# Batch statistics of a bottleneck's last convolution: a pass over its output against the Gram matrix of its input

## The chip, the cores and the metric

The kernel runs on one core of a Trainium2 chip. The metric is device time of one execution in microseconds (us). One execution of the kernel was also recorded by the hardware profiler; all rows below come from that one. Everything is computed in f32.

## The reference

Two residual blocks follow each other on x of shape 64 x 1024 x 14 x 14, each with parameters of its own. The reference of one block, cut to what matters:

```python
def _conv(x, w, b, stride, pad):
    y = jax.lax.conv_general_dilated(x, w, window_strides=(stride, stride), padding=[(pad, pad), (pad, pad)], dimension_numbers=('NCHW', 'OIHW', 'NCHW'))
    return y + b.reshape(1, -1, 1, 1)

def _bn(x, gamma, beta):
    mean = jnp.mean(x, axis=(0, 2, 3), keepdims=True)
    var = jnp.var(x, axis=(0, 2, 3), keepdims=True)
    xn = (x - mean) * jax.lax.rsqrt(var + EPS)
    return gamma.reshape(1, -1, 1, 1) * xn + beta.reshape(1, -1, 1, 1)

out = jax.nn.relu(_bn(_conv(x, w1, b1, 1, 0), g1, be1))     # 1x1, 1024 -> 256 channels
out = jax.nn.relu(_bn(_conv(out, w2, b2, 1, 1), g2, be2))   # 3x3, 256 -> 256
out = _bn(_conv(out, w3, b3, 1, 0), g3, be3)                # 1x1, 256 -> 1024
out = jax.nn.softplus(residual_scale)[0] * out
return jax.nn.relu(x + out)
```

Mean and variance are taken over all 64 x 14 x 14 = 12544 pixels of a channel, so a convolution must be finished for all images before its result can be normalized.

## The kernel before

Channels lie on the 128 partitions: the 1024 channels in 8 slots of a partition (CS), the 256 in 2 (MS). Images are taken two at a time, so that a tile has 392 pixels (PX) and there are 32 tiles (T). The 256 channels of all images stay in on-chip memory through a block, as tiles y0 to y31 that each stage rewrites in place. The 1024 channels of all images do not fit on chip.

A block goes through these stages, each a loop over the 32 tiles:

- conv1: 8 slots of x against w1, for two output slots. ScalarE moves the result out of PSUM with its bias into y (L92), VectorE takes its statistics (L93, one set per tile).
- conv2: ScalarE normalizes y into a padded tile (L99; three pad tiles in turn, NPAD), TensorE runs nine taps x two slots for each output slot (L108), ScalarE moves the result into y (L114), VectorE takes statistics (L115).
- norm2_conv3_stats: ScalarE normalizes y in place (L127), TensorE runs conv3 for all eight output slots (L120), and VectorE takes statistics straight out of PSUM (L129). The products themselves are dropped.
- residual: x is loaded again (SP's queue), conv3 runs once more (L120), VectorE multiplies it by the scale and adds x (L138), ScalarE adds the shift and applies the relu (L141), and POOL's queue stores the tile (L143): in the first block to a buffer in DRAM (mid), in the second to the output. In the first block each tile goes on into the next block's conv1 from where it lies.

Between two stages, affine aggregates the tiles' statistics (L158) and works out scale and shift in small operations (L160 to L177). x tiles share four buffers, PSUM is eight banks with one tile each. The order within an engine and all signals come from a scheduler that works on the program as written; it tracks which operation reads or writes which tile.

Of the kernel before, what the change touches and what calls it, by code (L numbers as in the profile page):

```python
"""Two ResNet bottleneck blocks (1x1 -> 3x3 -> 1x1 convolutions, each with batch statistics) in NCHW.

Channels lie on partitions: channel c of 1024 is partition c // 8, slot c % 8, and channel c of 256 is
partition c // 2, slot c % 2, so that an image's rows of a partition are contiguous in DRAM. The 256
channels of all images stay in SBUF through a block, a tile for every two images; each stage rewrites
these tiles in place. The last convolution runs twice: for its statistics, and again where its result
is added to the residual, as its 1024 channels do not fit on chip. Where the first block ends, its
result feeds the next block's first convolution straight from SBUF.
"""

# [1 line left out]

# [4 lines left out]

FP = mybir.dt.float32
AF = mybir.ActivationFunctionType
ALU = mybir.AluOpType  # L20

P = 128
N, C, H, W = 64, 1024, 14, 14
HW = H * W
M = 256  # channels between the 1x1 convolutions
CS = C // P  # slots of a partition with 1024 channels
MS = M // P  # and with 256
G = 2  # images in a tile
T = N // G
PX = G * HW  # L30
HP, WP = H + 2, W + 2
TAPS = [(i, j) for i in range(3) for j in range(3)]
EPS = 1e-5
NPAD = 3

# Columns of a block's packed parameters.
B1, G1, BE1, B2, G2, BE2 = (MS * i for i in range(6))
B3, G3, BE3 = (6 * MS + CS * i for i in range(3))
RS = 6 * MS + 3 * CS
NPAR = RS + 1  # L40


@with_exitstack
def bottlenecks(ctx: ExitStack, tc: tile.TileContext, x, w1s, w2s, w3s, pars, out):
    nc = tc.nc
# [3 lines left out]
    keep = ctx.enter_context(tc.tile_pool(name="keep", bufs=1))  # L49
    wpool = ctx.enter_context(tc.tile_pool(name="weights", bufs=1))  # L50
    xpool = ctx.enter_context(tc.tile_pool(name="x", bufs=4))
    small = ctx.enter_context(tc.tile_pool(name="small", bufs=2))
    psum = ctx.enter_context(tc.tile_pool(name="psum", bufs=8, space=bass.MemoryType.PSUM))
    dram = ctx.enter_context(tc.tile_pool(name="dram", bufs=1, space=bass.MemoryType.DRAM))

    ys = [keep.tile([P, MS, PX], FP, tag=f"y{t}", name=f"y{t}") for t in range(T)]
    pads = [keep.tile([P, MS, G, HP, WP], FP, tag=f"pad{i}", name=f"pad{i}") for i in range(NPAD)]
    mids = [dram.tile([P, G, CS * HW], FP, tag=f"mid{t}", name=f"mid{t}") for t in range(T)]

# [17 lines left out]
        nc.sync.dma_start(out=xt.rearrange("p i s f -> p i (s f)"), in_=x_t[t] if b == 0 else mids[t])  # L77
        return xt

    def psum_tile():  # L80
        return psum.tile([P, PX], FP, tag="ps", name="ps")

    def conv1(xt, t, w1, par, stats):
        for o in range(MS):
# [32 lines left out]
    def conv3(t, o, w3):  # L117
        ps = psum_tile()
        for s in range(MS):
            nc.tensor.matmul(ps, w3[:, s, o, :], ys[t][:, s, :], start=(s == 0), stop=(s == MS - 1))  # L120
        return ps

    def norm2_conv3_stats(t, w3, aff, stats):
        scale, shift = aff
        for s in range(MS):
            y = ys[t][:, s, :]
            nc.scalar.activation(y, y, AF.Relu, bias=shift[:, s : s + 1], scale=scale[:, s : s + 1])  # L127
        for o in range(CS):
            nc.vector.bn_stats(stats[:, o, t, :], conv3(t, o, w3))  # L129

    def residual(b, t, w3, aff):
        """relu(x + scale * conv3 + shift), in place of x."""
        scale, shift = aff
        xt = load_x(b, t)
        for o in range(CS):
            ps = conv3(t, o, w3)
            v = xt[:, :, o, :]
            nc.vector.scalar_tensor_tensor(  # L138
                v, ps.rearrange("p (i f) -> p i f", i=G), scale[:, o : o + 1], v, ALU.mult, ALU.add
            )  # L140
            nc.scalar.activation(v, v, AF.Relu, bias=shift[:, o : o + 1])  # L141
        to = mids[t] if b == 0 else out_t[t]
        nc.gpsimd.dma_start(out=to, in_=xt.rearrange("p i s f -> p i (s f)"))  # L143
        return xt

    def stats_tile(n, name):
        return keep.tile([P, n, T, nc.vector.BN_STATS_DIM], FP, tag=f"stats{n}", name=name)

    def affine(stats, n, par, g, be, conv_bias=None):
        """scale and shift with scale * y + shift = g * (y - mean) / sqrt(var + EPS) + be, for y  # L150
        with the statistics, or for y + conv_bias where that is given."""

        def tl(name):
            return small.tile([P, n], FP, tag=f"{name}{n}", name=name)

        mv = small.tile([P, n, nc.vector.BN_AGGR_DIM], FP, tag=f"mv{n}", name="mv")
        for o in range(n):
            nc.vector.bn_aggr(mv[:, o, :], stats[:, o, :, :].rearrange("p t f -> p (t f)"))  # L158
        v, sd, r, q = tl("v"), tl("sd"), tl("r"), tl("q")
        nc.vector.tensor_scalar(v, mv[:, :, 1], EPS, None, ALU.add)  # L160
        nc.scalar.activation(sd, v, AF.Sqrt)  # L161
        nc.vector.reciprocal(r, sd)
        # One Newton step on r = v ** -0.5.
        nc.vector.tensor_mul(q, r, r)
        nc.vector.tensor_mul(q, q, v)
        nc.vector.tensor_scalar(q, q, -0.5, 1.5, ALU.mult, ALU.add)
        nc.vector.tensor_mul(r, r, q)
        scale, shift, off = tl("scale"), tl("shift"), tl("off")
        nc.vector.tensor_mul(scale, r, par[:, g : g + n])
        if conv_bias is None:  # L170
            nc.vector.tensor_scalar(off, mv[:, :, 0], -1.0, None, ALU.mult)
        else:
            bias = par[:, conv_bias : conv_bias + n]
            nc.vector.tensor_add(off, mv[:, :, 0], bias)
            nc.vector.tensor_sub(off, bias, off)
        nc.vector.tensor_mul(shift, off, scale)
        nc.vector.tensor_add(shift, shift, par[:, be : be + n])  # L177
        return scale, shift

    def softplus(par):  # L180
        """max(a, 0) + log1p(exp(-|a|))"""
        a = par[:, RS : RS + 1]

        def tl(name):
            return small.tile([P, 1], FP, tag=name, name=name)

        u, w, l, d, z = tl("u"), tl("w"), tl("l"), tl("d"), tl("z")
        nc.vector.tensor_scalar(u, a, -1.0, None, ALU.mult)  # L188
        nc.vector.tensor_tensor(u, u, a, ALU.min)  # L189
        nc.scalar.activation(u, u, AF.Exp)  # L190
        # log1p(u) = log(w) * u / (w - 1) with w = 1 + u rounded, and u where w is 1.
        nc.vector.tensor_scalar(w, u, 1.0, None, ALU.add)
        nc.scalar.activation(l, w, AF.Ln)
        nc.vector.tensor_scalar(d, w, 1.0, None, ALU.subtract)
        nc.vector.tensor_scalar(z, d, 0.0, None, ALU.is_equal)
        nc.vector.tensor_add(d, d, z)
        nc.vector.reciprocal(d, d)
        nc.vector.tensor_mul(l, l, d)
        nc.vector.tensor_add(l, l, z)
        nc.vector.tensor_mul(l, l, u)  # L200
        sp = tl("sp")
        nc.vector.tensor_scalar(sp, a, 0.0, None, ALU.max)
        nc.vector.tensor_add(sp, sp, l)
        return sp

# [1 line left out]
    w1 = load_w1(0)  # L207
    par = []
    for b in range(2):
        p = keep.tile([P, NPAR], FP, tag=f"par{b}", name=f"par{b}")  # L210
        nc.scalar.dma_start(out=p, in_=pars[b])
        par.append(p)
    for pad in pads:
        nc.gpsimd.memset(pad, 0.0)  # L214

    stats1 = stats_tile(MS, "stats1_0")
    for t in range(T):
        conv1(load_x(0, t), t, w1, par[0], stats1)
        if t == 2:
            w2, w3 = load_w2(0), load_w3(0)  # L220
    w1 = load_w1(1)

    for b in range(2):
        pb = par[b]
        sp = softplus(pb)
        aff = affine(stats1, MS, pb, G1, BE1)
        stats2 = stats_tile(MS, f"stats2_{b}")
        for t in range(T):
            conv2(t, w2, pb, aff, stats2)

        aff = affine(stats2, MS, pb, G2, BE2)
        stats3 = stats_tile(CS, f"stats3_{b}")
        for t in range(T):
            norm2_conv3_stats(t, w3, aff, stats3)
        if b == 0:
            w2 = load_w2(1)

        aff = affine(stats3, CS, pb, G3, BE3, conv_bias=B3)
        for a in aff:
            nc.vector.tensor_scalar(a, a, sp, None, ALU.mult)  # L240
        if b == 1:
            for t in range(T):
                residual(b, t, w3, aff)
            return
        stats1 = stats_tile(MS, f"stats1_{b + 1}")
        ahead = residual(b, 0, w3, aff)
        for t in range(T):
            xt, ahead = ahead, residual(b, t + 1, w3, aff) if t + 1 < T else None
            conv1(xt, t, w1, par[b + 1], stats1)
        w3 = load_w3(b + 1)  # L250
# [35 lines left out]
```

## Time and profile before

| | |
|---|---|
| median of 3 runs | 3594.09 us (3593.11 to 3594.46) |
| span of the profiled execution | 3593.3 us |
| granted TensorE clock, mean | 0.996 |
| TensorE matmul busy | 3552.1 us (99%) |
| VectorE busy | 794.0 us (22%) |
| ScalarE busy | 635.1 us (18%) |
| HBM read, written | 163.09 MB, 102.76 MB |

Rows name an engine (PE is TensorE's matmuls, PEld its weight loads, DVE is VectorE, ACT is ScalarE, POOL is GpSimd, SP is SyncE), a line of the kernel, the operation and its operands by the program's names, as in out<-in. A group row gives, after the count, busy time and mean duration, then the idle time just before its instructions and what ended it. A timeline row begins with start and length in us. Matmuls overlap each other in TensorE, so the mean duration of one is longer than the distance between two.

### The profile page before, as it was taken

To read this page: it belongs to the slowest core of one execution; us is meant where nothing else is said; L and a number is where in the kernel's file an instruction comes from. 1 tells how busy PE (TensorE), PEld (TensorE's weight loads), DVE (VectorE), ACT (ScalarE), POOL (GpSimd) and SP (SyncE) were. 2 spreads that over 40 slices of the span, in tenths; PEclk is the share of its full clock that TensorE was granted. 3 is DMA by queue.
4 is the path that set the end of the run, shared out by engine and by line. 5 is a ranking of instruction groups with operands and counts; after the bars stand their busy time and mean duration, and the time that the engine had idled before them with its cause. 6 is when DMAs were issued, how large, how long until landed. Compare 5 with 4: busy or idle time off the path is not lost.

```text
span 3593.3 us, 24805 instructions
## 1 busy us (share of the span) xinstructions
PE 3552.1 (99%) x10752; PEld 2043.4 (57%) x10752; DVE 794.0 (22%) x1394; ACT 635.1 (18%) x1037; POOL 42.7 (1%) x71
## 2 busy tenths in 40 slices
PE   8999999999999999999999999999999999999998
PEld 5555555555555555555555555555555555555555
DVE  1111000000002444422322320000000034445444
ACT  1111011101104000222322221101111040003444
POOL 0000000000000000000000000000000000000000
PEclk9999999999999999999999999999999999999999
DMA  6444000000000000244333430000000000005886
GB/s 236 155 153 164 0 0 0 1 0 0 0 0 27 0 0 1 94 157 153 152 152 153 159 140 0 0 0 0 0 0 1 0 0 0 0 0 212 299 299 264
DMA packets 36589, 267.44 MB, mean 74 GB/s; under 512 B 2944, under 2 KB 2944, under 8 KB 27520
## 3 DMA queue, kind: packets, MB, share of 16 engines
q1 hardware_dynamic: 22592, 160.96, 12.6%
q0 software_dynamic: 13312, 102.76, 6.9%
q10 hardware_dynamic: 576, 2.14, 0.2%
q8 instruction: 84, 1.38, 0.2%
q14 instruction: 25, 0.20, 0.0%
HBM read 163.09 MB, written 102.76 MB: 74 GB/s over the span
## 4 chain that ended last, share of the span: by engine, by line
issue 90%; PE 9%; POOL 1%; DMA 0%; POOLq 0%
PE ps L87 9%; POOL out L143 1%; POOL mid L143 0%; DMA x<-in_x 0%; POOLq L143 0%; POOLq L280 0%
## 5 line engine op out<-in xcount | busy, mean ns | idle before, releaser
L108 PE MATMUL ps<-pad,w 128*128 128x392 f32 x4608 | 1522.7, 493 | 10.3 <-ACT pad L99 10.3
L120 PE MATMUL ps<-y,w 128*128 128x392 f32 x4096 | 1357.1, 493 | 10.3 <-ACT y L127 10.3
L108 PEld LDWEIGHTS ps<-pad,w 128*128 128x128 f32 x4608 | 873.4, 190 | 659.6 <-ACT pad L99 11.5
L120 PEld LDWEIGHTS ps<-y,w 128*128 128x128 f32 x4096 | 779.6, 190 | 582.9 <-ACT y L127 12.2
L87 PE MATMUL ps<-x,w 128*128 128x392 f32 x2048 | 682.3, 494 | 9.9 <-DMA x<-in_x 9.9
L87 PEld LDWEIGHTS ps<-x,w 128*128 128x128 f32 x2048 | 390.4, 191 | 296.0 <-issue 12.6
L115 DVE BATCH_NORM_STATS2 stats<-y 128x6 f32<-128x392 f32 x128 | 72.9, 569 | 1452.0 <-ACT y L114 1452.0
L138 DVE SCALAR_TENSOR_TENSOR x<-ps,scale,x 128x392 f32<-128x392 f32 x512 | 319.2, 625 | 328.8 <-PE ps L120 325.1
L141 ACT ACTIVATE x<-x,shift 128x392 f32<-128x392 f32 x512 | 317.5, 622 | 373.4 <-DVE x L138 373.3
L129 DVE BATCH_NORM_STATS2 stats<-ps 128x6 f32<-128x392 f32 x512 | 293.0, 572 | 376.6 <-PE ps L120 376.6
L114 ACT ACTIVATE y<-ps,par 128x392 f32<-128x392 f32 x128 | 75.2, 587 | 1060.4 <-PE ps L108 1060.4
L93 DVE BATCH_NORM_STATS2 stats<-y 128x6 f32<-128x392 f32 x128 | 72.8, 569 | 616.1 <-ACT y L92 616.1
L92 ACT ACTIVATE y<-ps,par 128x392 f32<-128x392 f32 x128 | 75.2, 587 | 577.0 <-PE ps L87 577.0
L99 ACT ACTIVATE pad<-y,shift,scale 128x392 f32<-128x392 f32 x128 | 89.8, 709 | 309.5 <-PE ps L108 306.2
L161 ACT ACTIVATE sd<-v 128x2 f32<-128x2 f32 (+1 forms) x6 | 1.2, 205 | 614.4 <-DVE v L160 614.4
L127 ACT ACTIVATE y<-y,shift,scale 128x392 f32<-128x392 f32 x128 | 77.6, 699 | 3.2 <-DVE shift L177 3.2
L143 POOL DMA_DIRECT2D mid<-x x32 | 17.2, 537 | 2095.1 <-ACT x L141 2095.1
L143 POOL DMA_DIRECT2D out<-x x32 | 22.6, 707 | 1446.5 <-ACT x L141 1446.5
L158 DVE BATCH_NORM_AGGREGATE mv<-stats 128x2 f32<-128x192 f32 x24 | 24.5, 1022 | 0.8
L188 DVE TENSOR_SCALAR u<-par 128x1 f32<-128x1 f32 x2 | 0.3, 154 | 11.7 <-DMA par<-in_par 11.7
L214 POOL MEMSET pad<- 128x1024 f32 x3 | 2.7, 952 | 0.3 <-POOLq L274 0.3
L190 ACT ACTIVATE u<-u 128x1 f32<-128x1 f32 x2 | 0.4, 202 | 8.7 <-DVE u L189 8.7
(33 smaller groups left out, 18.7 us busy)
## 6 DMA issues: line engine op xcount, KB each, us to landing
x<-in_x SPq DMA_DIRECT2D x64, 1568.0 KB, 6.5
mid<-x POOLq DMA_DIRECT2D x32, 1568.0 KB, 5.4
x<-mid SPq DMA_DIRECT2D x32, 1568.0 KB, 8.4
out<-x POOLq DMA_DIRECT2D x32, 1568.0 KB, 10.6
w<-in_w SPq DMA_DIRECT2D x2, 2304.0 KB, 14.9
w<-in_w ACTq DMA_DIRECT2D x2, 1024.0 KB, 7.2
w<-in_w SPq DMA_DIRECT2D x2, 1024.0 KB, 14.0
par<-in_par ACTq DMA_DIRECT2D x2, 18.5 KB, 9.5
```

The source lines that it names most:

```text
L87: nc.tensor.matmul(ps.rearrange("p (i f) -> p i f", i=G), w1[:, s, o, :], xt[:, :, s, :], start=(s == 0), stop=(s == CS - 1),)
L92: nc.scalar.activation(y, ps, AF.Identity, bias=par[:, B1 + o : B1 + o + 1])
L99: nc.scalar.activation(pad[:, s, :, 1 : H + 1, 1 : W + 1], ys[t][:, s, :].rearrange("p (i h w) -> p i h w", i=G, h=H), AF.Relu, bias=shift ...
L108: nc.tensor.matmul(ps.rearrange("p (i h w) -> p i h w", i=G, h=H), w2[:, s, k, o, :], pad[:, s, :, i : i + H, j : j + W], start=(s == 0 an ...
L114: nc.scalar.activation(y, ps, AF.Identity, bias=par[:, B2 + o : B2 + o + 1])
L115: nc.vector.bn_stats(stats[:, o, t, :], y)
L120: nc.tensor.matmul(ps, w3[:, s, o, :], ys[t][:, s, :], start=(s == 0), stop=(s == MS - 1))
L127: nc.scalar.activation(y, y, AF.Relu, bias=shift[:, s : s + 1], scale=scale[:, s : s + 1])
L129: nc.vector.bn_stats(stats[:, o, t, :], conv3(t, o, w3))
L138: nc.vector.scalar_tensor_tensor(v, ps.rearrange("p (i f) -> p i f", i=G), scale[:, o : o + 1], v, ALU.mult, ALU.add)
L141: nc.scalar.activation(v, v, AF.Relu, bias=shift[:, o : o + 1])
L143: nc.gpsimd.dma_start(out=to, in_=xt.rearrange("p i s f -> p i (s f)"))
```

## The change

The statistics of conv3 no longer come from running conv3. Its output is linear in its input z (the normalized, relu'd y), so the mean of an output channel is w . mean(z), and its variance is w' G w less the square of that, with G the 256 x 256 matrix of the mean products of z's channels. To keep the numbers small, a constant per channel, max(be2, 0), is first subtracted from z.

- gram: z is taken in 49 steps of 256 pixels. Each step transposes four blocks of 128 x 128 on TensorE into one PSUM tile (two chunks of 128 pixels, two slots), VectorE subtracts the constant on the way out of PSUM into one of four tiles zt, and two accumulated products a chunk follow: 257 columns (the first slot against everything and a column of ones) and 129 columns (the second slot against itself and the ones). The products of a step stand behind the transposes of the next.
- conv3_stats: G is scaled and moved out of PSUM, multiplied by w3 (six matmuls of 512 columns), by w3 again on VectorE, and summed over partitions with matmuls of one column; the means come from matmuls of two columns. The result takes the place of the aggregated statistics, and affine is otherwise as before.
- All y tiles become views of one tile, and there are two pads instead of three. The packed parameters grow by 256 columns (the constant along a row). Their identity and ones are set up on POOL at the start. A tile q of the statistics shares the four x buffers.

The core of the diff:

```diff
-NPAD = 3
+NPAD = 2
+NPX = N * HW
+CH = 2
+NT = NPX // (CH * P)
+NZT = 4
...
-    ys = [keep.tile([P, MS, PX], FP, tag=f"y{t}", name=f"y{t}") for t in range(T)]
+    y_all = keep.tile([P, MS, NPX], FP, tag="y", name="y")
+    ys = [y_all[:, :, t * PX : (t + 1) * PX] for t in range(T)]
+    zts = [keep.tile([P, CH, M + 1], FP, tag=f"zt{i}", name=f"zt{i}") for i in range(NZT)]
+    ident = keep.tile([P, P], FP, tag="ident", name="ident")
...
-    def norm2_conv3_stats(t, w3, aff, stats):
+    def norm2(t, aff):
         scale, shift = aff
         for s in range(MS):
             y = ys[t][:, s, :]
             nc.scalar.activation(y, y, AF.Relu, bias=shift[:, s : s + 1], scale=scale[:, s : s + 1])
+
+    def gram(aff, crow):
+        g0 = psum.tile([P, 512], FP, tag="ps", name="g0")[:, : M + 1]
+        g1 = psum.tile([P, 512], FP, tag="ps", name="g1")[:, : P + 1]
+        normed = 0
+
+        def products(k, zt):
+            for c in range(CH):
+                first, last = k == 0 and c == 0, k == NT - 1 and c == CH - 1
+                nc.tensor.matmul(g0, zt[:, c, 0:P], zt[:, c, :], start=first, stop=last)
+                nc.tensor.matmul(g1, zt[:, c, P:M], zt[:, c, P:], start=first, stop=last)
+
+        before = None
+        for k in range(NT):
+            while normed * PX < (k + 1) * CH * P:
+                norm2(normed, aff)
+                normed += 1
+            tp = psum_tile(CH * M)
+            for c in range(CH):
+                px = slice((k * CH + c) * P, (k * CH + c + 1) * P)
+                for s in range(MS):
+                    nc.tensor.transpose(tp[:, (c * MS + s) * P : (c * MS + s + 1) * P], y_all[:, s, px], ident)
+            zt = zts[k % NZT]
+            nc.vector.tensor_tensor(
+                zt[:, :, :M], tp.rearrange("p (c m) -> p c m", c=CH),
+                crow[:, None, :].to_broadcast([P, CH, M]), ALU.subtract,
+            )
+            if before is not None:
+                products(*before)
+            before = k, zt
+        products(*before)
+        return g0, g1
+
+    def conv3_stats(grams, w3, ccol, mv):
+        g0p, g1p = grams
...
+        nc.vector.tensor_scalar(g0, g0p, 1.0 / NPX, None, ALU.mult)
+        nc.scalar.activation(g1, g1p, AF.Copy, scale=1.0 / NPX)
+        nc.vector.tensor_scalar(off, g0[:, P:M], 2.0, None, ALU.mult)
...
+        half = CS // 2
+        q = xpool.tile([P, MS, C], FP, tag="x", name="q")
+        for h in range(2):
+            cols = slice(h * half, (h + 1) * half)
+            t0, t1 = psum_tile(half * P), psum_tile(half * P)
+            nc.tensor.matmul(t0, g0[:, 0:P], w3[:, 0, cols, :], start=True, stop=True)
+            nc.tensor.matmul(t1, off, w3[:, 0, cols, :], start=True, stop=False)
+            nc.tensor.matmul(t1, g1[:, 0:P], w3[:, 1, cols, :], start=False, stop=True)
+            for s, t in ((0, t0), (1, t1)):
+                nc.vector.tensor_mul(
+                    q[:, s, h * half * P : (h + 1) * half * P], t, w3[:, s, cols, :].rearrange("p o c -> p (o c)")
+                )
         for o in range(CS):
-            nc.vector.bn_stats(stats[:, o, t, :], conv3(t, o, w3))
+            for s in range(MS):
+                nc.tensor.matmul(quad[:, o, 0:2], w3[:, s, o, :], m[:, s, :], start=(s == 0), stop=(s == MS - 1))
+        for o in range(CS):
+            for s in range(MS):
+                nc.tensor.matmul(quad[:, o, 2:3], q[:, s, o * P : (o + 1) * P], ones, start=(s == 0), stop=(s == MS - 1))
...
-        aff = affine(stats2, MS, pb, G2, BE2)
-        stats3 = stats_tile(CS, f"stats3_{b}")
-        for t in range(T):
-            norm2_conv3_stats(t, w3, aff, stats3)
+        aff = affine(aggregate(stats2, MS), MS, pb, G2, BE2)
+        grams = gram(aff, crow)
         if b == 0:
             w2 = load_w2(1)
 
-        aff = affine(stats3, CS, pb, G3, BE3, conv_bias=B3)
+        mv3 = small.tile([P, CS, nc.vector.BN_AGGR_DIM], FP, tag="mv3", name="mv3")
+        conv3_stats(grams, w3, ccol, mv3)
+        aff = affine(mv3, CS, pb, G3, BE3, conv_bias=B3)
```

More of the change, by code (lines that the diff above doesn't have):

```diff
@@ L14 @@
 import concourse.tile as tile
-from concourse import mybir
+from concourse import masks, mybir
 from concourse._compat import with_exitstack
@@ L40 @@
 NPAR = RS + 1
+NROW = M
 @with_exitstack
@@ L78, in load_x, with psum_tile @@
         return xt
-    def psum_tile():
-        return psum.tile([P, PX], FP, tag="ps", name="ps")
+    def psum_tile(n=PX):
+        return psum.tile([P, 512], FP, tag="ps", name="ps")[:, :n]
     def conv1(xt, t, w1, par, stats):
@@ new lines, in conv3_stats @@
+    def conv3_stats(grams, w3, ccol, mv):
+        g0p, g1p = grams
+        g0 = keep.tile([P, M + 1], FP, tag="g0", name="g0")
+        g1 = keep.tile([P, P + 1], FP, tag="g1", name="g1")
+        off = keep.tile([P, P], FP, tag="goff", name="goff")
+        nc.vector.tensor_scalar(g0, g0p, 1.0 / NPX, None, ALU.mult)
+        nc.scalar.activation(g1, g1p, AF.Copy, scale=1.0 / NPX)
+        nc.vector.tensor_scalar(off, g0[:, P:M], 2.0, None, ALU.mult)
+        m = keep.tile([P, MS, 2], FP, tag="zmean", name="zmean")
+        for s, d in ((0, g0[:, M:]), (1, g1[:, P:])):
+            nc.vector.tensor_copy(m[:, s, 1:2], d)
+            nc.vector.tensor_add(m[:, s, 0:1], d, ccol[:, s : s + 1])
+        quad = psum_tile(3 * CS).rearrange("p (o k) -> p o k", k=3)
+        ones = keep.tile([P, 1], FP, tag="ones", name="ones")
+        nc.vector.memset(ones, 1.0)
+        half = CS // 2
[10 more added lines that the diff above has]
+                )
+        for o in range(CS):
+            for s in range(MS):
[3 more added lines that the diff above has]
+                nc.tensor.matmul(quad[:, o, 2:3], q[:, s, o * P : (o + 1) * P], ones, start=(s == 0), stop=(s == MS - 1))
+        r = small.tile([P, CS, 3], FP, tag="quad", name="quad")
+        nc.vector.tensor_copy(r, quad)
+        nc.vector.tensor_copy(mv[:, :, 0], r[:, :, 0])
+        sq = small.tile([P, CS], FP, tag="sq", name="sq")
+        nc.vector.tensor_mul(sq, r[:, :, 1], r[:, :, 1])
+        nc.vector.tensor_sub(mv[:, :, 1], r[:, :, 2], sq)
@@ L147, in stats_tile, with aggregate @@
         return keep.tile([P, n, T, nc.vector.BN_STATS_DIM], FP, tag=f"stats{n}", name=name)
-    def affine(stats, n, par, g, be, conv_bias=None):
-        def tl(name):
-            return small.tile([P, n], FP, tag=f"{name}{n}", name=name)
+    def aggregate(stats, n):
         mv = small.tile([P, n, nc.vector.BN_AGGR_DIM], FP, tag=f"mv{n}", name="mv")
@@ L158, in affine, with tl @@
             nc.vector.bn_aggr(mv[:, o, :], stats[:, o, :, :].rearrange("p t f -> p (t f)"))
+        return mv
+    def affine(mv, n, par, g, be, conv_bias=None):
+        def tl(name):
+            return small.tile([P, n], FP, tag=f"{name}{n}", name=name)
         v, sd, r, q = tl("v"), tl("sd"), tl("r"), tl("q")
@@ L209, in bottlenecks @@
     for b in range(2):
-        p = keep.tile([P, NPAR], FP, tag=f"par{b}", name=f"par{b}")
+        p = keep.tile([P, NPAR + NROW], FP, tag=f"par{b}", name=f"par{b}")
         nc.scalar.dma_start(out=p, in_=pars[b])
@@ L214, in bottlenecks @@
         nc.gpsimd.memset(pad, 0.0)
+    for zt in zts:
+        nc.gpsimd.memset(zt[:, :, M:], 1.0)
+    masks.make_identity(nc, ident)
     stats1 = stats_tile(MS, "stats1_0")
@@ L225, in bottlenecks @@
         sp = softplus(pb)
-        aff = affine(stats1, MS, pb, G1, BE1)
+        crow = keep.tile([P, M], FP, tag="crow", name="crow")
+        nc.vector.tensor_scalar(crow, pb[:, NPAR:], 0.0, None, ALU.max)
+        ccol = keep.tile([P, MS], FP, tag="ccol", name="ccol")
+        nc.vector.tensor_scalar(ccol, pb[:, BE2 : BE2 + MS], 0.0, None, ALU.max)
+        aff = affine(aggregate(stats1, MS), MS, pb, G1, BE1)
         stats2 = stats_tile(MS, f"stats2_{b}")
@@ L264, in packed @@
         cols.append(np.broadcast_to(get("residual_scale").reshape(1, 1), (P, 1)))
+        cols.append(np.broadcast_to(get("be2").reshape(P, MS).T.reshape(1, M), (P, M)))
         w1 = get("w1").reshape(P, MS, P, CS).transpose(2, 3, 1, 0)
```

## The prediction

> **What bounds the kernel now.** The page comes first: which engine is full, and whether it is full all the way.
>
> ```profile
> span 3593.3 us, 24805 instructions
> ...
> PE 3552.1 (99%) x10752; PEld 2043.4 (57%) x10752; DVE 794.0 (22%) x1394; ACT 635.1 (18%) x1037; POOL 42.7 (1%) x71
> ...
> PE   8999999999999999999999999999999999999998
> ```
>
> TensorE is busy in every slice, and no other engine passes 22%. Whatever leaves TensorE's list shortens the run, as long as no other engine is slow in the stage that takes its place. The waits say how little TensorE stands still:
>
> ```profile
> PE ps L120 <- ACT y L127: 10.3, 2, 5.2
> ...
> PE ps L108 <- ACT pad L99: 10.3, 2, 5.2
> PE ps L87 <- DMA x<-in_x: 9.9, 1, 9.9
> ```
>
> About 30 us in all: the first load, and four stage starts of 5.2 us each, at which the statistics of the stage before must be finished first. Then the busy time by stage; the third and the sixth stretch are the statistics passes of the two blocks, and the last is the second block's residual.
>
> ```profile
> 1117.00:1463.00 346.00, 341.41 (x1032) 196.98 (x1033) 156.85 (x276) 39.12 (x66) 0.00 (x0) 1.00 0.02 7
> ...
> 2915.00:3255.00 340.00, 340.00 (x1035) 196.24 (x1034) 157.38 (x280) 33.09 (x56) 0.00 (x0) 1.00 0.00 0
> 3255.00:3593.00 338.00, 327.56 (x996) 188.74 (x994) 156.06 (x250) 155.34 (x250) 22.61 (x32) 0.99 0.77 286
> ```
>
> The columns are length, busy time and instructions of PE, PEld, DVE, ACT and POOL, then the granted clock, the DMA share and GB/s. In a statistics pass TensorE is full and VectorE less than half full. The groups give its pieces:
>
> ```profile
> L120 PE MATMUL ps<-y,w 128*128 128x392 f32 x4096 | 1357.1, 493 | 10.3 <-ACT y L127 10.3
> L120 PEld LDWEIGHTS ps<-y,w 128*128 128x128 f32 x4096 | 779.6, 190 | 582.9 <-ACT y L127 12.2
> ...
> L138 DVE SCALAR_TENSOR_TENSOR x<-ps,scale,x 128x392 f32<-128x392 f32 x512 | 319.2, 625 | 328.8 <-PE ps L120 325.1
> ...
> L129 DVE BATCH_NORM_STATS2 stats<-ps 128x6 f32<-128x392 f32 x512 | 293.0, 572 | 376.6 <-PE ps L120 376.6
> L114 ACT ACTIVATE y<-ps,par 128x392 f32<-128x392 f32 x128 | 75.2, 587 | 1060.4 <-PE ps L108 1060.4
> ...
> L99 ACT ACTIVATE pad<-y,shift,scale 128x392 f32<-128x392 f32 x128 | 89.8, 709 | 309.5 <-PE ps L108 306.2
> ```
>
> L120 serves the statistics pass and the residual, in each of two blocks: 4 x 32 tiles x 8 outputs x 2 slots = 2048 matmuls in the code and 4096 records here. So one f32 matmul is two records, each with a weight load of its own. The mean of 493 ns is a latency; the pace comes from the timeline of an undisturbed stretch:
>
> ```profile
> 1120.82 19.46 ACT L127 ACTIVATE y<-y,shift,scale 128x392 f32<-128x392 f32 x32 [1.61 <-DVE shift L177]
> ...
> 1139.81 326.37 PE L120 MATMUL ps<-y,w 128*128 128x392 f32 x991
> ```
>
> 326.37 / 991 = 0.329 us for a record of 392 columns, that is 0.84 ns a column, and 0.493 - 0.329 = 0.16 us of latency that is hidden in a stream.
>
> **The change, part by part.**
>
> *Removed.* In each block 32 x 8 x 2 = 512 matmuls, 1024 records x 0.3293 = 337.2 us, all on the path. The 256 BATCH_NORM_STATS2 and 8 aggregations on VectorE go too, but they lie beside TensorE and are worth nothing.
>
> *Added: products.* 49 steps a block, each with two chunks of 128 pixels. A chunk has a product of 257 columns (two records of 257 x 0.84 = 0.216 us) and one of 129 (two of 0.108 us), if the weight load keeps up. All matmuls of the trace are long, so loads always hide. Two loads issued into an idle array show what a load by itself holds up:
>
> ```profile
> 2906.47 0.19 PEld L120 LDWEIGHTS ps<-y,w 128*128 128x128 f32 x1 [5.78 <-ACT y L127]
> ...
> 2906.47 0.30 PEld L120 LDWEIGHTS ps<-y,w 128*128 128x128 f32 x2 [5.78 <-ACT y L127]
> ```
>
> The second load ends 0.30 us after the start of the first and takes 0.19 itself, so it began 0.11 us after it: a load of 0.19 us lets the next begin after 0.11. I take 0.11 as the floor for a short record; the other end is the whole 0.19. Products per step: 4 x 0.216 + 4 x 0.11 = 1.30 us.
>
> *Added: transposes.* Four of 128x128 a step. No row shows one. The lower end is one record each with its load wholly hidden and at half a product's price by column, 128 x 0.84 / 2 = 0.054 us, a guess at the most that leaving the products out can save. The upper is two records at 0.19. I take one record at the load's 0.11, nearest to the row just shown, because moving values through the array has no sum of products that would have to be split: 0.44 us a step. If it is split like every f32 product here, it is 0.88.
>
> The Trainium skill, "TensorE: Matmul & The Clock Gate", Terms, says that transpose mode makes f32 four times faster on trn2. Against two records of 0.108 us that would be 0.054 us, below the floor of the load, so the sum by it would be the one taken here.
>
> *One step* is 1.30 + 0.44 = 1.74 us, and 49 steps are 85.5 us a block.
>
> *What lies beside it.* VectorE's one subtraction of 512 columns out of PSUM a step: six operations of 392 columns there, back to back, take
>
> ```profile
> 1463.46 0.17 DVE L160 TENSOR_SCALAR v<-mv 128x8 f32<-128x8 f32 x1
> ...
> 1465.75 3.40 DVE L138 SCALAR_TENSOR_TENSOR x<-ps,scale,x 128x392 f32<-128x392 f32 x6
> ```
>
> 0.57 us each. With 0.17 us of that fixed, as for the operation of 8 columns above them, and the rest 1.02 ns a column, 512 columns cost 0.69 us. The products of a step are issued after the next step's transposes, so the subtraction has 1.74 us for 0.16 (array) + 0.69: hidden. ScalarE's normalization runs at 19.46 / 32 = 0.61 us an operation, 1.22 a tile; a step needs 256 / 392 of one, 0.79 us: hidden too. If the step ran at half its length, VectorE would be late next.
>
> *Start of the stage.* Before, TensorE began behind the first normalization. Now the first products need two of them, a transpose and the subtraction, and the second transposes need the next tile, 2.4 us of ScalarE. I take 2 us more (0 to 4).
>
> *Tail, new on the path.* After the last product VectorE scales 257 columns (0.17 + 257 x 1.02 ns = 0.43, with the array's 0.16 and the signals some 0.8 us). Six products of 512 columns: 12 records x 0.43 = 5.2 us. Then 32 matmuls of one or two columns, 64 records at the floor of 0.11 = 7.0 us (12.1 at 0.19). VectorE's four multiplications of 512 columns trail by one and end under the mean's 32 records. Together 13.0 us. In these 7 us the array is nearly empty, and empty stretches are followed by a lower clock:
>
> ```profile
> 1118.00:1121.50 3.50, 0.00 (x0) 0.00 (x0) 2.31 (x11) 0.88 (x3) 0.00 (x0) 1.00 0.89 363
> 1122.00:1124.50 2.50, 2.50 (x5) 1.23 (x5) 0.00 (x0) 2.50 (x6) 0.00 (x0) 0.50 0.65 276
> ```
>
> I add 3 us (0 to 6): 16 us a block. The parameters of the affine follow, under the residual's matmuls: from the last aggregation (the row below) to the first residual operation at 1465.75 they took 2.3 us, and with four small operations ahead 3 us; seven free PSUM tiles x 4 records x 0.329 = 9.2 us cover them. Before, eight aggregations of about 1 us hid there in the same way.
>
> ```profile
> 1462.40 1.02 DVE L158 BATCH_NORM_AGGREGATE mv<-stats 128x2 f32<-128x192 f32 x1
> ```
>
> *At nothing.* Two pads instead of three: ScalarE needs 1.4 us for a pad, and the other pad's tile keeps TensorE for 36 x 2 x 0.329 = 23.7 us; without that cover it would be 1.4 us a tile. The tile q holds one of the four x buffers until the tail's end; three loads stay ahead, 31 us of residual (32 records a tile), against 8.4 us to land a load. Parameters of 149 KB (291 columns) instead of 18.5 KB on ScalarE's queue are needed at the first eviction, 16 records after the first x tile. Identity and ones on POOL precede no transfer that POOL issues before the residual. The second block's w2 stays in its place on SP's queue, and is needed a stage later.
>
> ```profile
> x<-mid SPq DMA_DIRECT2D x32, 1568.0 KB, 8.4
> ...
> par<-in_par ACTq DMA_DIRECT2D x2, 18.5 KB, 9.5
> ```
>
> All tiles are now views of one y. Were an access to wait for the whole tile, the stages would lose their overlap. What is there now waits by region:
>
> ```profile
> 707.65 0.72 ACT L99 ACTIVATE pad<-y,shift,scale 128x392 f32<-128x392 f32 x1 [5.28 <-PE ps L108]
> 713.63 0.59 ACT L114 ACTIVATE y<-ps,par 128x392 f32<-128x392 f32 x1 [5.27 <-PE ps L108]
> ```
>
> The first slot of a pad is rewritten 6 us before the last product that reads its second slot, and a pad is one tile.
>
> *Sum.* A block gives 337.2 - 85.5 - 2 - 16 = 233.7 us, two give 467.4. The profiled span 3593.3 becomes 3125.9; the median of the runs, 3594.09, lies 0.8 above the span, so 3127.
>
> **The rivals.**
>
> *Transposes in two records* (0.88 a step): 98 x 0.44 = 43 us more, 3170. For it: every f32 product in the trace is two records. Against: it multiplies nothing.
>
> *The weight load's whole 0.19 is the pace* of every short record: 8 x 0.08 a step, 98 x 0.64 = 62, and 10 in the tails: 3199. For it: L120's load rows. Against: the two loads 0.11 apart. With two-record transposes besides, 1.51 + 0.76 + 0.86 = 3.13 us a step, 3273.
>
> *Turning from transposes to products and back empties the array*: the latency of 0.16 us, twice a step, 196 x 0.16 = 32, 3159. The trace has nothing that turns so.
>
> *The clock falls in the new stage*: at half clock a step is 3.48 us, 171 more, 3298. For it: the row of 0.50 above; against: that followed 5 us of nothing, and here 1.3 of 1.74 us are dense products.
> The Trainium skill speaks for it: the same page, Part 4, says that transposes do not count as activity for the full clock, and has about 275 ns for one in a kernel. By that figure, as an estimate, the steps would be 98 x 4 x 0.165 = 65 us longer, 3192.
>
> *One y tile makes accesses wait for each other*: in the 3x3 stage each tile's pad would wait for the eviction before it, 0.16 + 0.59 + 0.71 = 1.46 us x 64 = 93, and in the first block's residual 0.75 x 31 = 23: 3243. Against: the pad rows.
>
> *Slower than before*: VectorE's subtraction, with an operand repeated by a zero step, becomes the bound. It decides from (337.2 - 18) / 49 = 6.5 us for each, against 0.69; nothing on VectorE here with 392 columns takes over 0.63.
>
> **How the numbers follow.** The forecast 0.50, with 3095 to 3150 as its own range (transposes wholly hidden, no loss of clock or start, to 0.23 us of friction a step); two-record transposes 0.15; the load's pace 0.12; turning 0.10; the one tile 0.05; half clock or slow transposes 0.04; both of load and records 0.03; slower 0.01. The range 3090 to 3225 holds the first four. About 0.2% is what a measurement of this kernel tells from no change, and every case but the last lies far outside of it.
>
> **What would show it.** Right: 4 x 49 x 2 transposes as as many records, steps 1.7 to 1.8 us apart in the timeline, VectorE's subtractions with idle time before each that a transpose ends, 13 to 18 us from the last long product to the residual's first, clock 1.00 in the new stage, and the 3x3 stages as long as before. Wrong: twice the transpose records, load starts 0.19 apart, TensorE waiting for VectorE or ScalarE, or TensorE idle between tiles of the 3x3 stage.

## The result, and the profile after

The changed kernel takes 3132.96 us (median of 4 runs, 3132.32 to 3133.71) against 3593.99 us beside it: a ratio of 0.8717, 95% interval 0.8705 to 0.8729. The profiled span is 3130.5 us; 3125.9 were forecast for it. On the page of the changed kernel TensorE is full as before:

```profile
span 3130.5 us, 23038 instructions
...
PE 3088.2 (99%) x10032; PEld 1845.2 (59%) x10032; DVE 563.9 (18%) x998; ACT 636.5 (20%) x1039; POOL 42.4 (1%) x76
...
PE   8999999999999999999999999999999999999998
PEld 5555555555555577555555555555555555875554
```

The two humps in the row of the weight loads are the new stages, whose short products have a load each. The groups give their pieces:

```profile
L120 PE MATMUL ps<-pad,w 128*128 128x392 f32 x4608 | 1520.9, 493 | 10.3 <-ACT pad L111 10.3
...
L132 PE MATMUL ps<-y,w 128*128 128x392 f32 x2048 | 686.7, 496 | 0.0
...
L151 PE MATMUL g<-zt 128*128 128x257 f32 x392 | 119.7, 387 | 0.0
L165 DVE TENSOR_TENSOR zt<-ps,crow 128x512 f32<-128x512 f32 x98 | 67.9, 693 | 108.5 <-PE ps L163 108.3
...
L152 PE MATMUL g<-zt 128*128 128x129 f32 x392 | 76.3, 277 | 0.0
L163 PE MATMUL ps<-ident,y 128*128 128x128 f32 x392 | 61.8, 282 | 10.4 <-issue 5.2
```

Half of L120's 4096 records of before are gone (now L132 with 2048). The transposes (L163) are 392 = 98 steps x 4, one record each, the products (L151, L152) 392 each, two records each. The 3x3 stage has the busy time it had (1520.9 against 1522.7 us). One step in the timeline of the first block:

```profile
1203.06 0.47 PEld L163 LDWEIGHTS ps<-ident,y 128*128 128x128 f32 x4
1203.17 0.60 PE L163 MATMUL ps<-ident,y 128*128 128x128 f32 x4
1203.50 0.30 PEld L151 LDWEIGHTS g<-zt 128*128 128x128 f32 x2
1203.60 0.60 PE L151 MATMUL g<-zt 128*128 128x257 f32 x2
1203.81 0.69 DVE L165 TENSOR_TENSOR zt<-ps,crow 128x512 f32<-128x512 f32 x1 [1.06 <-PE ps L163]
...
1204.81 0.47 PEld L163 LDWEIGHTS ps<-ident,y 128*128 128x128 f32 x4
```

The next step's transposes begin 1.75 us later; four of them hold TensorE for 1203.50 - 1203.06 = 0.44 us. VectorE works 0.69 us and stands idle for 1.06. Then the tail of the statistics:

```profile
1209.51 0.38 PE L152 MATMUL g<-zt 128*128 128x129 f32 x2
...
1210.20 1.12 PE L197 MATMUL ps<-w,g 128*128 128x512 f32 x2 [0.30 <-DVE g L181]
...
1215.45 3.66 PE L206 MATMUL ps<-zmean,w 128*128 128x2 f32 x32
...
1218.97 3.98 PE L209 MATMUL ps<-ones,q 128*128 128x1 f32 x18
...
1222.81 1.66 PE L132 MATMUL ps<-y,w 128*128 128x392 f32 x2
...
1224.26 2.98 PE L209 MATMUL ps<-ones,q 128*128 128x1 f32 x14
...
1227.10 13.15 PE L132 MATMUL ps<-y,w 128*128 128x392 f32 x31
```

The first 32 small records (L206) take 1218.97 - 1215.45 = 3.52 us, 0.11 each. The other 32 (L209) load as many columns and stream one, but take 0.20 to 0.21 each (the last 14 of them 1227.10 - 1224.26 = 2.84 us): the clock has fallen, and it is still down when the residual begins. By stretches (length, busy times, then clock, DMA share and GB/s):

```profile
1215.45:1218.90 3.45, 3.45 (x33) 3.45 (x31) 0.69 (x1) 0.00 (x0) 0.00 (x0) 1.00 0.00 0
1218.95:1227.00 8.05, 8.05 (x36) 7.42 (x35) 0.00 (x0) 0.00 (x0) 0.00 (x0) 0.50 0.00 0
1227.10:1232.50 5.40, 5.40 (x10) 2.87 (x11) 3.75 (x20) 1.26 (x3) 0.00 (x0) 0.50 0.77 271
1233.00:1240.00 7.00, 7.00 (x23) 4.03 (x22) 3.16 (x6) 3.11 (x5) 0.00 (x0) 1.00 0.01 4
```

A busy share of 100% in a row of PE says nothing of the speed; the clock column does. These 13.5 us at half clock come in each block (in the second from 2772.0 to 2785.6).

### The profile page after: what moved, and what is told of

It reads as the page before. It is cut to its first block, busy times and chain, and to the rows that moved or that the text cites. A ratio compares the mean times of both kernels' runs of the same rounds, so it can differ in the third digit from the quotient of the medians.

```text
span 3130.5 us, 23038 instructions
## 1 busy us (share of the span) xinstructions
PE 3088.2 (99%) x10032; PEld 1845.2 (59%) x10032; DVE 563.9 (18%) x998; ACT 636.5 (20%) x1039; POOL 42.4 (1%) x76
## 4 chain that ended last, share of the span: by engine, by line
PE 59%; issue 39%; POOL 1%; DMA 1%; DVE 0%; POOLq 0%; ACT 0%; SPq 0%; ACTq 0%
PE ps L120 24%; PE ps L99 21%; PE ps L132 11%; PE g L151 1%; PE ps L163 1%; PE g L152 1%; POOL out L229 1%; DMA x<-mid 0%; DMA x<-in_x 0%; PE ps L209 0%; PE ps L206 0%; PE ps L197 0%; PE ps L199 0%; PE ps L198 0%; POOLq L229 0%
## 5 line engine op out<-in xcount | busy, mean ns | idle before, releaser
L120 PE MATMUL ps<-pad,w 128*128 128x392 f32 x4608 | 1520.9, 493 | 10.3 <-ACT pad L111 10.3
L120 PEld LDWEIGHTS ps<-pad,w 128*128 128x128 f32 x4608 | 872.5, 189 | 658.7 <-ACT pad L111 11.5
L132 PE MATMUL ps<-y,w 128*128 128x392 f32 x2048 | 686.7, 496 | 0.0
L132 PEld LDWEIGHTS ps<-y,w 128*128 128x128 f32 x2048 | 391.9, 192 | 286.6 <-issue 4.7
L151 PE MATMUL g<-zt 128*128 128x257 f32 x392 | 119.7, 387 | 0.0
L165 DVE TENSOR_TENSOR zt<-ps,crow 128x512 f32<-128x512 f32 x98 | 67.9, 693 | 108.5 <-PE ps L163 108.3
L152 PEld LDWEIGHTS g<-zt 128*128 128x128 f32 x392 | 75.2, 192 | 11.4
L152 PE MATMUL g<-zt 128*128 128x129 f32 x392 | 76.3, 277 | 0.0
L163 PE MATMUL ps<-ident,y 128*128 128x128 f32 x392 | 61.8, 282 | 10.4 <-issue 5.2
L151 PEld LDWEIGHTS g<-zt 128*128 128x128 f32 x392 | 60.6, 195 | 0.6 <-DVE zt L165 0.6
L163 PEld LDWEIGHTS ps<-ident,y 128*128 128x128 f32 x392 | 47.7, 146 | 12.8 <-ACT y L139 7.0
## 6 DMA issues: line engine op xcount, KB each, us to landing
par<-in_par ACTq DMA_DIRECT2D x2, 146.5 KB, 10.2
```

Of the source, the lines that this page charges most:

```text
L120: nc.tensor.matmul(ps.rearrange("p (i h w) -> p i h w", i=G, h=H), w2[:, s, k, o, :], pad[:, s, :, i : i + H, j : j + W], start=(s == 0 an ...
L151: nc.tensor.matmul(g0, zt[:, c, 0:P], zt[:, c, :], start=first, stop=last)
L152: nc.tensor.matmul(g1, zt[:, c, P:M], zt[:, c, P:], start=first, stop=last)
L163: nc.tensor.transpose(tp[:, (c * MS + s) * P : (c * MS + s + 1) * P], y_all[:, s, px], ident)
```

## The experiments

Theory: the stage is a sum of TensorE records that nothing else delays, and what is lost beyond it is the clock in the tail. Rivals: views of one y tile wait for each other, VectorE already sets the step, transpose mode has a price of its own, or the clock falls for what comes before the tail.

**One y tile and two pads alone.** The kernel before with

```diff
-NPAD = 3
+NPAD = 2
-    ys = [keep.tile([P, MS, PX], FP, tag=f"y{t}", name=f"y{t}") for t in range(T)]
+    y_all = keep.tile([P, MS, N * HW], FP, tag="y", name="y")
+    ys = [y_all[:, :, t * PX : (t + 1) * PX] for t in range(T)]
```

> The kernel before with one part of the change alone: all y tiles as views of one tile, and two pads instead of three; the statistics pass stays. Theory (accesses wait by region, and one spare pad is enough): 3594 us as before, within 3. Rival (accesses to one tile wait for each other): 93 us more in the two 3x3 stages and 23 in the first block's residual, 3710, with TensorE idle some 1.4 us before each tile of the 3x3 stage. Rival on the pads alone (a pad comes free too late): 1.4 us a tile, 64 tiles, 3684.

Measured: 3594.71 us against 3594.28, ratio 1.0001 (0.9991 to 1.001). TensorE's waits on ScalarE are those of before, four stage starts:

```profile
PE ps L121 <- ACT y L128: 10.3, 2, 5.2
...
PE ps L109 <- ACT pad L100: 10.3, 2, 5.2
```

The layout costs and gives nothing; all of the gain is the new statistics.

**Transposes as ordinary products.**

```diff
-                    nc.tensor.transpose(tp[...], y_all[:, s, px], ident)
+                    nc.tensor.matmul(tp[...], y_all[:, s, px], ident, start=True, stop=True)
```

> The changed kernel with its transposes as ordinary f32 products with the identity, without transpose mode; same numbers. Theory (the mode saves one of two records, and a short record costs 0.11 us whatever it does): four records more a step, 98 x 4 x 0.11 = 43 us more, 3176 against 3133, steps 2.18 to 2.2 us apart, clock 1.00 in the steps. Rival (the mode has a price of its own, in turning the array from transposes to products and back, or in the clock): the four records are partly paid for by what no longer has to turn, under 25 us more, below 3158. Rival (f32 products of 128 columns cost more than the load, at the load row's 0.19): eight records at 0.19 against four at 0.11, 106 us more, 3239.

Measured: 3174.53 us (ratio 0.8832, 0.8818 to 0.8845), 41.6 us more than the changed kernel.

```profile
1201.07 0.97 PEld L163 LDWEIGHTS ps<-ident,y 128*128 128x128 f32 x8
...
1203.28 0.97 PEld L163 LDWEIGHTS ps<-ident,y 128*128 128x128 f32 x8
```

Eight records a step in place of four, steps 2.21 us apart in place of 1.75: (2.21 - 1.75) x 98 = 45 us by these two rows, 41.6 by the time. So transpose mode saves one of two records. The 3 us between the two figures are no price of turning: in the recorded run with plain products the clock is at 0.50 for 3.2 us of the first block's new stage (6.2 in the changed kernel), and for 10.2 us in and behind the second block's tail in place of 13.6. That is some 6.4 us less at half speed, half of which is time.

**Half the pixels in each transpose.**

```diff
+                    n = P if k < 8 else P // 2
-                    nc.tensor.transpose(tp[...], y_all[:, s, px], ident)
+                    nc.tensor.transpose(tp[:n, ...], y_all[:, s, px.start : px.start + n], ident)
```

and the subtraction on n partitions: from the ninth step on, half of the pixels are left out of the statistics.

> From the ninth step on, each transpose takes only 64 of its 128 pixels: 64 stationary columns to load instead of 128, the same 128 columns of identity to stream, and the subtraction on 64 partitions. The other 64 pixels of a chunk are left out of the statistics (old values stand in their place), so it does part of the computation. Theory (a transpose is paid by its weight load, 0.11 us for 128 columns): half the load, 0.055 us less each, 41 steps x 2 blocks x 4 x 0.055 = 18 us less, 3115; transposes 0.055 to 0.06 us apart. Rival (a transpose is paid by streaming its 128 columns, at the 0.84 ns a column of a product's record, 0.108 us): no change, 3133, transposes still 0.11 us apart.

Measured: 3132.33 us (ratio 0.8715, 0.8702 to 0.8728): no change. The rows of one step:

```profile
1200.91 0.44 PEld L164 LDWEIGHTS ps<-ident,y 128*64 128x64 f32 x4
1201.02 0.60 PE L164 MATMUL ps<-ident,y 128*64 128x128 f32 x4
1201.35 0.30 PEld L151 LDWEIGHTS g<-zt 128*128 128x128 f32 x2
```

Four transposes hold TensorE for 0.44 us with half the load. The theory that the load pays them falls, unless a load is dear whatever its columns. The next run asks that.

**The mean's small matmuls with half the columns to load, twice as many.**

```diff
-        for o in range(CS):
-            for s in range(MS):
-                nc.tensor.matmul(quad[:, o, 0:2], w3[:, s, o, :], m[:, s, :], ...)
+        for a in (0, P // 2):
+            for o in range(CS):
+                for s in range(MS):
+                    nc.tensor.matmul(quad[a : a + P // 2, o, 0:2], w3[:, s, o, a : a + P // 2], m[:, s, :], ...)
```

> The changed kernel with each small matmul of the means taken as two, each with 64 of the 128 stationary columns; the same result from twice as many records, all of the lower half first. Read from the distances in the trace before the clock falls. Theory (0.11 us is the load, and goes with the columns loaded): 64 records of 0.054 us, 3.5 us as before. Rival (a record with a load of its own cannot be under 0.108 us, whatever it loads or streams): 64 records of 0.108, 6.9 us. If the theory holds, the transposes with half the load, which stayed 0.11 us apart, were paid by the columns they stream; if the rival holds, what pays a transpose stays open between the two. The time: 3133 or 3137 to 3150, by the clock.

Measured, in a single run (3134.03 us):

```profile
1216.97 3.60 PEld L207 LDWEIGHTS ps<-zmean,w 128*64 128x64 f32 x64 [0.76 <-issue]
1220.59 3.91 PEld L213 LDWEIGHTS ps<-ones,q 128*128 128x128 f32 x18
```

64 records in 3.62 us, 0.057 each. So a load does go with its columns, 0.11 us for 128 and 0.057 for 64, where it is what a record waits for. The transposes with 64 loaded columns could have gone at that pace and did not: this speaks for the 128 columns they stream, at 0.11 / 128 = 0.86 ns a column, a product record's 0.84. No run streamed fewer columns through a transpose, so a fixed price of the same size is not excluded.

**One zt tile.** Products written right behind their subtraction, and

```diff
-NZT = 4
+NZT = 1
```

> One zt tile instead of four, and the products of a step written behind its own subtraction: the subtraction can only begin when the products before it are through, while the transposes still run ahead. It takes away the cover under which the subtraction stands. Theory (the subtraction of 0.69 us is hidden, and costs itself, the array's 0.16 and about 0.1 of signals when it is not): a step is 1.30 + 0.16 + 0.69 + 0.1 = 2.25 us in place of 1.75, 98 x 0.5 = 49 us more, 3182, with TensorE idle before each step's first product. Rival (VectorE already sets the step, by a wait that the rows put down to TensorE): little changes, within 10 of 3133.

Measured: 3192.31 us (ratio 0.8882, 0.8867 to 0.8897), 59.4 more than the changed kernel; 49 were expected.

```profile
1200.00 0.70 PE L151 MATMUL g<-zt 128*128 128x257 f32 x2 [0.35 <-DVE zt L164]
...
1201.62 0.69 DVE L164 TENSOR_TENSOR zt<-ps,crow 128x512 f32<-128x512 f32 x1 [1.67 <-PE g L152]
1202.36 0.30 PEld L151 LDWEIGHTS g<-zt 128*128 128x128 f32 x2 [0.59 <-DVE zt L164]
```

Now the subtraction waits for the last product and the next product for the subtraction; a step is 2.36 us, 0.61 more, and 98 x 0.61 = 60. The 0.1 us over the 2.25 assumed is the weight load of the first product, which nothing hides now: its two records take 0.70 us here and 0.60 in the changed kernel. In the changed kernel this is all hidden: VectorE does not set the step there.

**A mixed tail.** Four of the residual's first eight results are computed inside the statistics' tail, and the residual takes them over (those lines are not shown):

```diff
     def conv3_stats(grams, w3, ccol, mv):
+        ahead = [conv3(0, 0, w3)]
...
         for o in range(CS):
+            if o == half:
+                ahead.append(conv3(0, 1, w3))
             for s in range(MS):
                 nc.tensor.matmul(quad[:, o, 0:2], ...)
         for o in range(CS):
+            if o % half == 0:
+                ahead.append(conv3(0, 2 + o // half, w3))
             for s in range(MS):
                 nc.tensor.matmul(quad[:, o, 2:3], ...)
```

> The changed kernel with four of the first residual tile's eight last-convolution results moved up into the tail of the statistics: one before the six products of 512 columns, one between the two halves of the mean's small matmuls, one before and one in the middle of the sums' small matmuls. The work is the same, only its order on TensorE. Theory (the clock falls to half because some 3.4 us of small matmuls leave the array empty, and stays there for 13.7 us of a block): no stretch of small matmuls is longer than 1.8 us, the clock stays at 1.00, which gives back 0.107 us for each of the sums' 32 records and 2.7 us of the residual's first tile, and the first result also stands in the 0.6 us in which TensorE waits for VectorE: 2 x (3.4 + 2.7 + 0.6) = 13 us less, 3120. Rival (the clock falls for what came before, 90 us of steps with transposes in them, or falls at any rate at this place): at most the 0.6 us twice, 3132, and the clock still 0.50 after the small matmuls.

Measured: 3118.34 us (3117.39 to 3119.06; ratio 0.8675, 0.8663 to 0.8687), 14.6 less than the changed kernel; 13 were expected.

```profile
1216.99 1.84 PE L209 MATMUL ps<-zmean,w 128*128 128x2 f32 x16
1218.69 1.56 PE L132 MATMUL ps<-y,w 128*128 128x392 f32 x4
...
1226.30 1.84 PE L214 MATMUL ps<-ones,q 128*128 128x1 f32 x16
1228.00 16.05 PE L132 MATMUL ps<-y,w 128*128 128x392 f32 x48
```

```profile
1210.50:1228.00 17.50, 17.50 (x94) 12.40 (x93) 3.85 (x11) 0.28 (x1) 0.00 (x0) 1.00 0.00 0
```

All small records now take (1228.00 - 1226.30) / 16 = 0.106 us and the clock is 1.00 through the tail and after it. The same steps stand before it, so the clock had not fallen for them. The mixed tail also fills the 0.5 us in which TensorE waits ahead of the six products, but short waits alone do not bring the clock down. In the run with one zt tile, TensorE waits 0.35 us in every step, and the clock stays:

```profile
1130.00:1208.00 78.00, 67.22 (x406) 55.91 (x405) 22.87 (x33) 27.93 (x47) 0.00 (x0) 1.00 0.05 19
```

It falls for the long run of small matmuls.

**The mean's matmuls first.** The same small matmuls in two stretches with the six large products between them.

```diff
+        [the loop of the mean's matmuls]
         for h in range(2):
             t0, t1 = psum_tile(half * P), psum_tile(half * P)
...
-        [the loop of the mean's matmuls]
```

> The changed kernel with the mean's small matmuls (32 records of two columns) ahead of the six products of 512 columns instead of behind them; the sums' 32 records of one column stay at the end. The small matmuls are as many, but in two stretches of 3.5 us with 5 us of full products between them. Theory (a stretch of empty array has to fill one window of about 3.4 us, and windows run on a grid of their own): each stretch alone covers a whole window rarely, so the clock falls later or not at all: 0 to 12 us less, 3121 to 3133; the clock falls in a shorter stretch than the 13.7 us of a block. But the wait for the mean's four small VectorE operations, 0.5 us, comes to lie on the path. Rival (the clock falls for what came before): 3133 to 3135, with the clock falling at the same distance from the last step.

Measured: 3124.15 us (ratio 0.8693, 0.8681 to 0.8705), 8.8 less. The clock still falls behind the first stretch, in both blocks and not rarely, but for 3.4 us in place of 13.5, and full products follow there (the first of the six had slipped in ahead of these 30 records). It does not fall behind the second, of which the longest piece is 18 records, 1222.71 - 1220.79 = 1.9 us:

```profile
1211.45:1214.70 3.25, 3.25 (x31) 3.25 (x30) 0.69 (x1) 0.00 (x0) 0.00 (x0) 1.00 0.00 0
1214.90:1218.30 3.40, 3.40 (x5) 1.32 (x5) 0.00 (x0) 0.00 (x0) 0.00 (x0) 0.50 0.00 0
1218.40:1230.00 11.60, 11.60 (x56) 7.80 (x56) 5.72 (x24) 0.76 (x3) 0.00 (x0) 1.00 0.27 90
```

```profile
1220.79 2.06 PE L209 MATMUL ps<-ones,q 128*128 128x1 f32 x18
1222.71 1.56 PE L132 MATMUL ps<-y,w 128*128 128x392 f32 x4
```

**The changed kernel again**, beside the last one.

> The changed kernel once more, beside the two below: 3133 us.

Measured: 3132.24 us (ratio 0.8713, 0.8701 to 0.8725).

**The mixed tail with one sum less.**

```diff
+            qh = slice(h * half * P, (h + 1) * half * P)
+            nc.vector.tensor_add(q[:, 0, qh], q[:, 0, qh], q[:, 1, qh])
...
-            for s in range(MS):
-                nc.tensor.matmul(quad[:, o, 2:3], q[:, s, o * P : (o + 1) * P], ones, start=(s == 0), stop=(s == MS - 1))
+            nc.tensor.matmul(quad[:, o, 2:3], q[:, 0, o * P : (o + 1) * P], ones, start=True, stop=True)
```

> The changed kernel with the mixed tail, and the two slots of q added on VectorE before the sums over partitions, so that these take 8 small matmuls in place of 16. Theory (small matmuls cost 0.108 us a record on the path, VectorE is idle there and ends before them): 16 records x 0.108 x 2 = 3.5 us less than the mixed tail, 3115. Rival (the sums now wait for VectorE): the last addition ends about 0.17 + 0.69 + 0.69 after the last of the six products, under the 4 us of means and residual results, so it would have to be twice as slow: 3118 or more.

Measured: 3114.55 us (3113.91 to 3115.03; ratio 0.8664, 0.8652 to 0.8676), 17.7 less than the changed kernel beside it and 3.8 less than the mixed tail in its own comparison. VectorE is through before the sums begin:

```profile
1217.43 0.69 DVE L206 TENSOR_TENSOR q<-q 128x512 f32<-128x512 f32 x1
...
1222.71 0.95 PE L215 MATMUL ps<-ones,q 128*128 128x1 f32 x8
```

It is the fastest kernel of this study.

## Why the prediction was right, step by step

- *Removed, 337.2 us a block*: right. L132 keeps 2048 records without a wait.
- *Products, 1.30 us a step*: right. 1204.81 - 1203.50 = 1.31.
- *Transposes, 0.44 us a step*: the number was right, and the reason half wrong. One record each, as argued. But the runs speak for the streamed columns as the price (128 x 0.84 ns = 0.108 us), not the load's floor of 0.11; at 128 columns the two are the same. Of what the Trainium skill, "TensorE: Matmul & The Clock Gate", states, the fourfold speed (Terms) is not what the runs show: by the run with plain products a transpose costs half of a product, 0.11 against 0.22 us. The 275 ns of its Part 4 nearly come back here as the length of a record (a mean of 282 ns in L163's row), but not as what one costs in a stream, 0.11 us. The clock, on which that part also speaks, is 1.00 in the steps:

```profile
1130.00:1208.00 78.00, 78.00 (x537) 73.08 (x535) 31.19 (x45) 28.57 (x48) 0.00 (x0) 1.00 0.06 23
```

Transposes hold TensorE for only a quarter of this time (0.44 of 1.75 us), so whether they count as activity for the clock stays open.
- *Beside it*: right; shown by the run with one zt tile, in which the cover is gone and costs 59 us.
- *Start, 2 us more a block*: nearly right in size. From the first load to the fourth step's transposes it is 1127.77 - 1120.51 = 7.26 us, with three groups of transposes and two of products between (12 + 16 = 28 loads): 3 x 0.44 + 2 x 1.31 = 3.94, so 3.3 are lost.

```profile
1120.51 0.29 PEld L163 LDWEIGHTS ps<-ident,y 128*128 128x128 f32 x2 [5.81 <-issue]
...
1127.77 0.47 PEld L163 LDWEIGHTS ps<-ident,y 128*128 128x128 f32 x4
```

```profile
1120.50:1127.77 7.27, 7.23 (x27) 5.84 (x28) 2.08 (x3) 7.27 (x13) 0.00 (x0) 0.57 0.98 413
```

Before, 50 records from 1121.59 to 1139.81 (the last of the row's 51 begins there) took 18.22 us in place of 16.5, 1.8 lost:

```profile
1121.59 18.72 PE L120 MATMUL ps<-y,w 128*128 128x392 f32 x51 [5.16 <-ACT y L127]
```

So the start costs 1.6 us more here, and 1.3 in the second block by the same count. But the cause named, waiting for the normalization, is the small part: the clock is at 0.50 until 1126.7, which alone is some 3.1 of the 3.3. Why it lasts 6.2 us here stays open; with plain products it was 3.2.
- *Tail, 16 us a block*: the term that was mis-sized. Its parts by the full clock held: 0.5 us of wait, 5.25 for the six products, 3.5 for the mean's 32 records. The clock took more than the 3 us allowed for it, and than the 6 of its range: 32 sums at 0.21 in place of 0.11, 3.2 us; two residual records among them, 1224.26 - 1222.81 - 0.66 = 0.8; and 5.4 us of residual at half speed, 2.7 us. That is 6.7 in all. From the last product's end (1209.51 + 2 x 0.11) to the residual's stream it is 17.4, less 0.66 for the two residual records, plus 2.7: 19.4 a block.
- *The sum*: 2 x (-0.6 for the start + 0.3 for the steps + 3.4 for the tail) = +6.2. The span is only 4.6 over the forecast, and that is in part luck. From the first matmul of the statistics to the first of the next 3x3 stage, and in the second block to the last of the kernel, the traces shrink by (2139.81 - 1121.59) - (1908.63 - 1120.54) = 230.1 and (3582.56 - 2906.47) - (3119.75 - 2674.02) = 230.4 us. Both together fall 6.9 short of twice 233.7. The other 2.3 us were gained in stages that the change leaves alone; 1.3 of them only because the half clock at the start of the second 3x3 stage lasted 5.7 us in the recorded run of before and 3.2 in that of the changed kernel:

```profile
2139.80:2145.50 5.70, 5.69 (x9) 3.15 (x10) 0.00 (x0) 2.99 (x5) 0.00 (x0) 0.50 0.06 23
...
1908.60:1911.80 3.20, 3.17 (x5) 1.85 (x6) 0.00 (x0) 1.79 (x3) 0.00 (x0) 0.50 0.11 47
```

The medians of all runs differ by 461.0 us, 6.4 short of the forecast 467.4.
- *At nothing*: right for the pads and the one y tile by a run of their own. The q tile, the larger parameters and the POOL operations were not tried alone; of the 6.9 us the sum leaves 0.7 for all of them together.

## What to carry to other kernels

Where statistics of a linear map are wanted, the moments of its smaller input can stand for a full pass over its output; price it by records, with the streamed columns and the loaded columns each as a floor, and write the next step's transposes ahead of this step's products so that the copy out of PSUM hides. Look at the clock column wherever TensorE's matmuls are tiny: a row that is 100% busy can run at half speed and hand that speed on to the stage behind it. Spread such matmuls between full ones that need nothing from them.

## What the runs showed of the hardware

- Back-to-back matmuls of one or two columns did not hold the clock: it was 1.00 for the first 3.5 us of them and 0.50 afterwards, for 13.5 us, and it stayed at 1.00 where no such stretch was longer than 1.9 us. One of 3.3 us was enough for 3.4 us at half clock. What lies between 1.9 and 3.3 us was not tried.
- At a stage's start, behind 5 us of idle TensorE, the half clock lasted for 3.2 to 6.2 us of work in these traces, not always the same at the same place. A difference of some 1.5 us between two recorded runs can be no more than that.
- A weight load that nothing hides costs by its columns: 0.11 us for 128, 0.057 for 64.
- An f32 transpose of 128 x 128 is one record where an f32 product is two, and takes a product record's 0.11 us, whether 128 or 64 columns are loaded for it. Why its load is recorded shorter (0.14 us against 0.19) stays open; it changed no time here.
